# Layer 0's attention scores: float32r halves stacked over 128 rows, or float32 products on 32-row quarters

## The chip, the cores and the metric

The kernel runs on one core of one Trainium2 chip. The metric is the device time of one execution in microseconds. The kernel before was run three times: median 3027.15 us, 3026.36 to 3032.22. The profile is of one more execution, of 3024.22 us.

## What is computed

The input is x of 2 images, 256 channels, 64 x 64 points (4096 positions). Two layers follow one another, each with a group normalisation ahead of it and its result added to its input. The change touches layer 0 alone: an attention of 8 heads with 32 channels each over all 4096 positions.

```
qkv = einsum('bchw,oc->bohw', x, qkv_w) + qkv_b      # x: normalised
q, k, v = qkv.reshape(b, 3, 8, 32, 4096) ...
attn_logits  = einsum('bhci,bhcj->bhij', q, k) / sqrt(32)
attn_weights = softmax(attn_logits, axis=-1)
out = einsum('bhij,bhcj->bhci', attn_weights, v)
```

Layer 1 (windowed attentions, a 3 x 3 convolution) is the same in both kernels.

## The kernel before

**Stages.** For each image b: `project0` (L424) makes queries, keys and values on TensorE and puts them into DRAM; `attention0` (L494) is layer 0's attention; then layer 1. TensorE's, ScalarE's and VectorE's (DVE's) order inside `attention0` is the order in which the program writes the instructions (`manual_schedule`).

**Groups, blocks, units.** The attention of one image has 16 groups g: head h = g // 2, and half p = g % 2 of the 4096 queries. A group goes over 32 blocks j of 128 keys. For one block there are four units u of 512 queries each. A unit is one tile of scores, 128 keys by 512 queries, and there are 2048 units per image.

**Scores.** `heads4` (L426) writes each query and key twice to DRAM: rounded to float32r (ScalarE), and what the rounding left over (DVE, L439). `fetch_head` (L401) lays both parts of the keys over four row quarters of 32 partitions, `fetch_queries` (L411) both parts of the queries, so that one float32r product with 128 rows of contraction sums all four part-products. `scores` (L558) does nine units at a time in groups of 1, 1, 3, 2 and 2 (`PHASE`), each unit into one bank of a ring of seven PSUM banks; ScalarE takes the exponential of each group in one instruction (L573) into a ring of 28 places in SBUF. `touch` (L528) tells the scheduler which banks do not overlap.

**Weighted sums.** `quarters` (L578, matmul at L582) multiplies one block's exponentials with its values: four products of 32 output columns, one for each unit, onto four column quarters of the array, into the 32-partition quarters of one bank `av`. All blocks but the first and the last are done in two steps of 256 columns. These are plain float32.

**Row sums of the exponentials.** DVE adds each block's exponentials to two running tiles (`add_rows`, L597, addition at L619). For seven blocks of a group (`SUMMED`, L480) the addition is made by DMAs that accumulate in memory instead (`add_in_memory`, L621, issued by GpSimd at L627 and L629), and DVE adds their result at the start of the next group (L832). At a group's end `sum_rows` (L643) sums over the partitions by a product with ones into a spare bank of the ring; for the last group of an image the last four blocks are also summed so.

**Finish.** `finish` (L654) copies the row sums out (ScalarE, L660), takes their reciprocal through DRAM, and multiplies the copied weighted sums (ScalarE copy, L846). It is taken up at later blocks of the next group (`steps`, L810).

**Order.** The loop at the end of `attention0` puts out nine scores, then as many half-block steps of weighted sums as keep the ring in balance, then nine scores again.

Of the kernel before, what the change touches and what calls it, by code (L numbers as in the profile page):

```python
# [18 lines left out]
P = 128  # L19
# [22 lines left out]
def direct_layers(ctx: ExitStack, tc: tile.TileContext, a: dict, out: bass.AP, bad: bass.AP):  # L42
# [338 lines left out]
    def normalise(dst, src, k, mean, rstd):  # L381
# [9 lines left out]
    halves = {  # L391
        nm: [dram.tile([2, C, N], F32, name=f"{nm}_halves_{b}") for b in range(B)] for nm in ("wq0", "wk0")
    }
# [7 lines left out]
    def fetch_head(b, h, held):  # L401
        r = slice(HD0 * h, HD0 * h + HD0)
        kt = kpool.tile([P, N], F32R, tag="kv", name=f"k_{b}_{h}")
        for g in range(4):
            nc.sync.dma_start(
                out=kt[HD0 * g : HD0 * g + HD0, :].bitcast(F32), in_=halves["wk0"][b][g // 2, r, :]
            )
        held["k", h] = kt
        nc.sync.dma_start(out=held["v"][:, h % 2, :, :], in_=vals[b][:, :, r])

    def fetch_queries(b, g, held):  # L411
        h, p = divmod(g, 2)
        r = slice(HD0 * h, HD0 * h + HD0)
        for w in range(2):
            qt = w4([P, 2, T], f"q_{b}_{g}_{w}", F32R)
            n0 = (4 * p + 2 * w) * T
            for q in range(4):
                nc.sync.dma_start(
                    out=qt[HD0 * q : HD0 * q + HD0].rearrange("p s n -> p (s n)").bitcast(F32),
                    in_=halves["wq0"][b][q % 2, r, n0 : n0 + 2 * T],  # L420
                )
            held["q", g, w] = qt

    def project0(b, xn, w0):  # L424

        def heads4(nm, g):  # L426
            for t in range(NT):
                nt = f"{nm}_{b}_{g}_{t}"
                n = slice(t * T, (t + 1) * T)
                final = b > 0 and (nm, g, t) == ("wq0", KC - 1, NT - 1)  # L430
                pq = bank([P, T], f"p_{nt}", at=7 if final else None)
                for k in range(KC):
                    nc.tensor.matmul(  # L433
                        pq, w0[nm][:, k, g * P : (g + 1) * P], xn[:, k, n], start=k == 0, stop=k == KC - 1
                    )
                pair = w4([P, 2, T], f"hl_{nt}", F32R)
                bias = b0[nm][:, g : g + 1]
                nc.scalar.activation(pair[:, 0, :], pq, AF.Identity, bias=bias)
                nc.vector.scalar_tensor_tensor(  # L439
                    pair[:, 1, :], pq, bias, pair[:, 0, :].bitcast(F32), ALU.add, ALU.subtract  # L440
                )
                nc.sync.dma_start(
                    out=halves[nm][b][:, g * P : (g + 1) * P, n].rearrange("s p n -> p s n"),
                    in_=pair.bitcast(F32),
                )
# [3 lines left out]
        for i in range(N // P // 4):  # L449
# [19 lines left out]
            "acc": place[:, n_v + n_es : n_v + n_es + T].unsqueeze(1),  # L469
        }  # L470
        fetch_head(b, 0, held)
        fetch_queries(b, 0, held)
# [5 lines left out]
    RING, RING_A = 28, 17  # L478

    SUMMED = (3, 7, 11, 15, 18, 22, 26)  # L480

    def summed(g):

        return SUMMED if g else SUMMED[1:]


# [5 lines left out]
    RING_SHIFT = 3  # L492

    def attention0(b, xts, held):  # L494
# [5 lines left out]
        es = apool.tile([P, RING_A + 1, T], F32, tag="A", name=f"es_{b}")  # L500
        pair = cpool.tile([P, 2, T], F32, tag="col", name=f"acc_{b}")

        acc = [es[:, RING_A, :], held["acc"][:, 0, :], pair[:, 0, :], pair[:, 1, :]]
        vals2 = held["v"]
        n_units = NH0 * 2 * NJ * 4
        sums, added, copied = {}, {}, {}
        waiting = []
        last = NH0 * 2 - 1

        places = []  # L510
        n_places = 0

        def at_places(first, n):

            while n > 0:
                at = (first + RING_SHIFT) % RING
                m = min(n, (RING_A if at < RING_A else RING) - at)
                yield m, es[:, at : at + m, :] if at < RING_A else held["es"][:, at - RING_A : at - RING_A + m, :]
                first, n = first + m, n - m

        BANKS = 7

        PHASE = (1, 1, 3, 2, 2)
        recent, spare = [], [0]
        rows_made = ([], [])
        ring = psum["sc"].tile([P, BANKS, T], F32, tag="ring", name=f"ring_{b}")

        def touch(made, banks):  # L528

            for engine, past, other in recent:
                if engine != made.ins.engine and not banks & other:
                    tc.declare_no_dep(made.ins, past.ins, reason="another bank of the ring")
            recent.append((made.ins.engine, made, banks))
            del recent[:-60]
            return made

        def touch_spare(made):
            return touch(made, {spare[0]})  # L540

        def spare_bank():

            nonlocal n_places
            n_places += 1
            spare[0] = (n_places - 1) % BANKS
            return ring[:, spare[0], :]

        def runs_of(n):

            at = n_places
            while n > 0:
                e = (at + RING_SHIFT) % RING
                m = min(n, BANKS - at % BANKS, (RING_A if e < RING_A else RING) - e)
                yield at, m
                at, n = at + m, n - m

        def scores():  # L558

            nonlocal n_places  # L560
            for size in PHASE:
                for at, m in list(runs_of(min(size, n_units - len(places)))):
                    sc = ring[:, at % BANKS : at % BANKS + m, :]
                    for i in range(m):
                        unit = len(places) + i
                        g, (j, u) = unit // (4 * NJ), divmod(unit % (4 * NJ), 4)
                        touch(nc.tensor.matmul(  # L567
                            sc[:, i, :], held["k", g // 2][:, j * P : (j + 1) * P], held["q", g, u // 2][:, u % 2, :],
                            start=True, stop=True,
                        ), {at % BANKS + i})  # L570
                    ((_, dst),) = at_places(at, m)
                    touch(
                        nc.scalar.activation(dst, sc, AF.Exp, scale=SC0), set(range(at % BANKS, at % BANKS + m))  # L573
                    )
                    places.extend(range(at, at + m))
                    n_places = at + m

        def quarters(dst, lhs, rhs, start, stop, part=None, note=lambda made: made):  # L578

            n = slice(0, T) if part is None else slice(part * T // 2, (part + 1) * T // 2)  # L580
            for u in range(4):
                note(nc.tensor.matmul(dst[HD0 * u : HD0 * u + HD0, n], lhs, rhs(u)[:, n], start=start, stop=stop))  # L582

        def unit(g, j, u):
            ((_, e),) = at_places(places[(g * NJ + j) * 4 + u], 1)
            return e[:, 0, :]

        def two_units(g, j, w):

            one, two = (places[(g * NJ + j) * 4 + 2 * w + s] for s in range(2))  # L590
            if two == one + 1:
                runs = list(at_places(one, 2))
                if len(runs) == 1:
                    return [(slice(0, 2), runs[0][1])]
            return [(slice(s, s + 1), unit(g, j, 2 * w + s).unsqueeze(1)) for s in range(2)]

        def add_rows(g, j):  # L597
            if j == 0:
                sums[g] = psum["av"].tile([P, T], F32, tag="av", name=f"av_{b}_{g}")
                added[g] = [w4([P, 2, T], f"e_{b}_{g}_{w}") for w in range(2)]  # L600
                return
            for w in range(2):
                dst = added[g][w]
                if j in summed(g):
                    if w == 0:
                        add_in_memory(g, j)
                    continue
                if j == 1:
                    first = two_units(g, 0, w), two_units(g, 1, w)
                    if len(first[0]) == len(first[1]) == 1:  # L610
                        nc.vector.tensor_add(dst, first[0][0][1], first[1][0][1])
                    else:
                        for s in range(2):
                            nc.vector.tensor_add(dst[:, s, :], unit(g, 0, 2 * w + s), unit(g, 1, 2 * w + s))
                    continue
                for s, src in two_units(g, j, w):
                    if g == last and j in SUMMED_LAST:
                        continue
                    nc.vector.tensor_add(dst[:, s, :], dst[:, s, :], src)  # L619

        def add_in_memory(g, j):  # L621
            assert not waiting or j != summed(g)[0]
            runs = [(acc[u].unsqueeze(1), unit(g, j, u).unsqueeze(1)) for u in (0, 1)]
            runs += [(pair[:, s, :], src) for s, src in two_units(g, j, 1)]
            for dst, src in runs:
                if j == summed(g)[0]:
                    nc.gpsimd.dma_start(out=dst, in_=src)  # L627
# [1497 lines left out]
```

## Time and profile before

| what | value |
|---|---|
| median of 3 runs | 3027.15 us |
| profiled execution | 3024.22 us |
| its span on the core | 3022.4 us |
| attention of image 0, first score to last weighted sum | 111.46 to 1132.29 us |
| attention of image 1 | 1607.40 to 2633.80 us |
| TensorE clock granted | 0.998 of full speed |

The page of a profile gives first each engine's busy time, then the chain of work that ended last (shares of the span), then the costliest groups of instructions: line, engine, operation, output and inputs, shape (of a matmul first rows times columns of the array that it uses), count, busy time and mean ns of one, then idle time before them. PE is TensorE, PEld its weight loads, ACT is ScalarE, POOL is GpSimd. TensorE's ends are modelled, so the starts tell more than the busy time. A float32 product has two records there, a float32r product one.

### The profile page before, as it was taken

Reading aid. Unit: us, or ns where it says so; the run is one execution under the profiler, and the core shown is the slowest. Engines: PE = TensorE matmul, PEld = TensorE weight load, DVE = VectorE, ACT = ScalarE, POOL = GpSimd, SP = SyncE. Lnnn points to the kernel's source line nnn. Section 1 sums busy time; section 2 is a strip of 40 time slices with the busy share of each in tenths; the row PEclk is TensorE's granted clock in tenths of the full one; section 3 lists DMA queues with packets and bytes.
Section 4 is the critical chain, followed back from the end, with each engine's and each line's share of the span. In section 5 each row is a group of like instructions: output and inputs, shape, how many; then the busy total and the mean of one; then the engine's idle time right before and its main releaser. Section 6 shows DMA issues by size and latency. Waiting matters only on the chain.

```text
span 3022.4 us, 64069 instructions
## 1 busy us (share of the span) xinstructions
PE 2963.0 (98%) x25161; PEld 1850.1 (61%) x25161; DVE 2443.4 (81%) x3111; ACT 2341.5 (77%) x3288; POOL 843.3 (28%) x930
## 2 busy tenths in 40 slices
PE   7999999999999999999999999999999999999998
PEld 4565556665565656577765555666555565576765
DVE  4698998999899999856647989989988899935543
ACT  2699999999999994622237999999999999844333
POOL 1022222322223230065401223222222222306440
PEclk9999999999999999999999999999999999999999
DMA  7979779897897761230169688797888976700000
GB/s 263 278 138 183 148 158 173 158 185 155 169 179 156 157 137 36 76 141 31 49 222 265 131 172 166 158 178 148 172 169 161 185 159 128 175 13 4 22 15 23
DMA packets 246662, 425.55 MB, mean 141 GB/s; under 512 B 99096, under 2 KB 110156, under 8 KB 244172
## 3 DMA queue, kind: packets, MB, share of 16 engines
q0 software_dynamic: 96960, 237.57, 40.8%
q1 hardware_dynamic: 149244, 183.51, 22.0%
q8 instruction: 199, 3.26, 0.5%
q14 instruction: 115, 0.94, 0.1%
q10 hardware_dynamic: 144, 0.26, 0.0%
HBM read 120.08 MB, written 68.39 MB: 62 GB/s over the span
## 4 chain that ended last, share of the span: by engine, by line
PE 87%; DVE 5%; DMA 3%; ACT 2%; issue 1%; SPq 0%; ACTq 0%; DVEq 0%; POOLq 0%
PE ring L567 32%; PE av L582 29%; PE mm L1036 7%; PE p_wk L433 2%; PE pv L456 2%; PE p_wq L433 2%; DVE prep L957 2%; PE prq_sr L1417 2%; PE prk_sr L1417 2%; PE pvs_sr L1106 2%; PE phk_sr L1406 1%; PE phq_sr L1406 1%; PE ring L582 1%; PE pvs_lr L1106 1%; PE py L1243 1%
## 5 line engine op out<-in xcount | busy, mean ns | idle before, releaser
L573 ACT ACTIVATE es<-ring 128x512 f32<-128x512 f32 (+2 forms) x1574 | 1202.3, 909 | 35.4 <-PE ring L567 23.3
L567 PE MATMUL ring<-q,k 128*128 128x512 f32 x4096 | 1083.9, 407 | 7.3 <-ACT es L573 5.4
L619 DVE TENSOR_TENSOR e<-e,es 128x1024 f32<-128x1024 f32 (+1 forms) x942 | 1028.8, 1153 | 28.4 <-ACT es L573 27.4
L567 PEld LDWEIGHTS ring<-q,k 128*128 128x128 f32 x4096 | 731.2, 188 | 382.7 <-ACT es L573 116.4
L573 ACT ACTIVATE v<-ring 128x512 f32<-128x512 f32 (+2 forms) x1036 | 785.6, 896 | 15.6 <-PE ring L567 7.5
L582 PE MATMUL av<-es,v 128*32 128x256 f32 (+1 forms) x9648 | 722.1, 389 | 0.0
L619 DVE TENSOR_TENSOR e<-e,v 128x1024 f32<-128x1024 f32 (+1 forms) x624 | 669.1, 1128 | 18.3 <-ACT v L573 17.6
L582 PE MATMUL av<-v 128*32 128x256 f32 x6224 | 506.0, 389 | 0.0
L582 PEld LDWEIGHTS av<-es,v 128*32 128x32 f32 x9648 | 325.2, 109 | 263.8 <-issue 105.1
L582 PEld LDWEIGHTS av<-v 128*32 128x32 f32 x6224 | 222.2, 109 | 169.8 <-issue 70.3
L1036 PE MATMUL mm<-v,wf 128*128 128x256 f32 x1024 | 227.6, 380 | 2.0 <-DVE z L1047 2.0
L629 POOL DMA_DIRECT2D es<-es x116 | 99.0, 853 | 438.5 <-ACT es L573 412.7
L1036 PEld LDWEIGHTS mm<-v,wf 128*128 128x128 f32 x1024 | 192.9, 190 | 33.7 <-issue 6.9
L1026 POOL TENSOR_TENSOR v<-col 128x512 f32<-128x512 f32 x128 | 165.3, 1317 | 172.8 <-ACT rk_sr L1195 40.3
L629 POOL DMA_DIRECT2D acc<-es x126 | 129.5, 1033 | 116.4 <-ACT es L573 32.1
L1043 ACT COPY z<-mm 128x512 f32<-128x512 f32 x32 | 18.7, 585 | 179.1 <-PE mm L1036 179.1
L627 POOL DMA_DIRECT2D es<-es x20 | 11.4, 568 | 508.6 <-ACT es L573 241.1
L629 POOL DMA_DIRECT2D es<-v x74 | 63.1, 853 | 291.1 <-ACT v L573 265.6
L1044 DVE TENSOR_TENSOR z<-z,mm 128x512 f32<-128x512 f32 x32 | 21.9, 686 | 125.3 <-ACT z L1043 124.9
L629 POOL DMA_DIRECT2D v<-es x114 | 115.3, 1011 | 24.7 <-ACT es L573 8.9
L629 POOL DMA_DIRECT2D acc<-v x86 | 87.5, 1017 | 81.9 <-DMA acc<-es 35.5
L1022 POOL TENSOR_TENSOR col<-xp 128x1152 f32<-128x1152 f32 x32 | 69.3, 2165 | 66.6 <-DVE xp L1487 55.4
(252 smaller groups left out, 2639.2 us busy)
## 6 DMA issues: line engine op xcount, KB each, us to landing
acc<-es POOLq DMA_DIRECT2D x122, 512.0 KB, 6.3
acc<-v POOLq DMA_DIRECT2D x78, 512.0 KB, 6.2
es<-es POOLq DMA_DIRECT2D x136, 256.0 KB, 4.2
v<-es POOLq DMA_DIRECT2D x134, 256.0 KB, 5.3
k<-wk_halves SPq DMA_DIRECT2D x64, 512.0 KB
q<-wq_halves SPq DMA_DIRECT2D x256, 128.0 KB
v<-v POOLq DMA_DIRECT2D x88, 256.0 KB, 4.8
es<-v POOLq DMA_DIRECT2D x86, 256.0 KB, 3.9
```

Source lines behind the costliest of these rows:

```text
L433: nc.tensor.matmul(pq, w0[nm][:, k, g * P : (g + 1) * P], xn[:, k, n], start=k == 0, stop=k == KC - 1)
L456: nc.tensor.matmul(pv[:, j, :], xn[:, k, n0 : n0 + P], w0["wv0"][:, k, :], start=k == 0, stop=k == KC - 1)
L567: touch(nc.tensor.matmul(sc[:, i, :], held["k", g // 2][:, j * P : (j + 1) * P], held["q", g, u // 2][:, u % 2, :], start=True, stop=True, ...
L573: nc.scalar.activation(dst, sc, AF.Exp, scale=SC0), set(range(at % BANKS, at % BANKS + m))
L582: note(nc.tensor.matmul(dst[HD0 * u : HD0 * u + HD0, n], lhs, rhs(u)[:, n], start=start, stop=stop))
L619: nc.vector.tensor_add(dst[:, s, :], dst[:, s, :], src)
L629: nc.gpsimd.dma_start(out=dst, in_=src, accum_op=ALU.add)
L1022: (nc.gpsimd.tensor_add if plus else nc.gpsimd.tensor_sub)(col, cols(one), cols(two))
L1026: (nc.gpsimd.tensor_add if plus else nc.gpsimd.tensor_sub)(dst, rows(one), rows(two))
L1036: nc.tensor.matmul(mm[:, m, r, :], wf[:, k, 4 * r + q, m * P : (m + 1) * P], v[r // 2][:, r % 2, k, :], start=k == 0, stop=k == KC - 1,)
L1106: nc.tensor.matmul(pv[:, i, :], tokens(c, 2 * half + i), wv[:, c, :], start=c == 0, stop=c == KC - 1)
L1417: nc.tensor.matmul(pr[m], wts[two][:, k, m * P : (m + 1) * P], hid[:, k, :], start=k == 0, stop=k == KC - 1)
```

## The change

The scores become plain float32 products with 32 rows of contraction. `heads4` writes queries and keys once, ScalarE and DVE in turn, in pairs of 512 columns. `fetch_head` lays the same 32 key rows on all four row quarters, and on quarter u the queries of unit u, for both halves of the queries at once; `fetch_queries` is gone. `scores` does runs of three units, each unit on its row quarter and into its own bank, alternately into two PSUM tiles of three banks, with one exponential per run. The ring in SBUF has 30 places in fixed order.

The accumulating DMAs are gone. For 11 of 32 blocks (7 in an image's last group) TensorE adds the row sums, by products with ones like the weighted sums, into a bank of their own, `rows`; DVE adds the other blocks as before. The copies out of the weighted and the row sums move from ScalarE to DVE. The loop puts out one run of three, then up to 2.2 steps on average, while there are steps to take.

```diff
     def fetch_head(b, h, held):
...
-        kt = kpool.tile([P, N], F32R, tag="kv", name=f"k_{b}_{h}")
-        for g in range(4):
+        kt = kpool.tile([P, N], F32, tag="kv", name=f"k_{b}_{h}")
+        qt = w4([P, 2, T], f"q_{b}_{h}")
+        for u in range(4):
+            rows = slice(HD0 * u, HD0 * u + HD0)
+            nc.sync.dma_start(out=kt[rows, :], in_=heads["wk0"][b][r, :])
             nc.sync.dma_start(
-                out=kt[HD0 * g : HD0 * g + HD0, :].bitcast(F32), in_=halves["wk0"][b][g // 2, r, :]
+                out=qt[rows], in_=heads["wq0"][b][r, :].rearrange("c (p u n) -> c p u n", p=2, u=4)[:, :, u, :]
             )
...
-                pair = w4([P, 2, T], f"hl_{nt}", F32R)
+                if t % 2 == 0:
+                    pair = w4([P, 2, T], f"pair_{nt}")
                 bias = b0[nm][:, g : g + 1]
-                nc.scalar.activation(pair[:, 0, :], pq, AF.Identity, bias=bias)
-                nc.vector.scalar_tensor_tensor(
-                    pair[:, 1, :], pq, bias, pair[:, 0, :].bitcast(F32), ALU.add, ALU.subtract
-                )
...
+                if t % 2 == 0:
+                    nc.scalar.activation(pair[:, 0, :], pq, AF.Identity, bias=bias)
+                else:
+                    nc.vector.tensor_scalar(pair[:, 1, :], pq, bias, None, ALU.add)
...
-    RING, RING_A = 28, 17
-    SUMMED = (3, 7, 11, 15, 18, 22, 26)
+    RING, RING_A = 30, 18
+    RING_SHIFT = 18
+    RUN = 3
...
+    def by_ones(g):
+        return (14, 16, 18, 20, 22, 24, 26) if g == NH0 * 2 - 1 else (6, 9, 11, 14, 16, 19, 21, 24, 26, 30, 31)
...
+        runs = [psum["sc"].tile([P, RUN, T], F32, tag=f"run{i}", name=f"run{i}_{b}") for i in range(2)]
...
+        def scores(i):
+            sc, first = runs[i % 2], RUN * i
+            n = min(RUN, n_units - first)
+            for s in range(n):
+                g, (j, u) = (first + s) // (4 * NJ), divmod((first + s) % (4 * NJ), 4)
+                rows = slice(HD0 * u, HD0 * u + HD0)
+                nc.tensor.matmul(
+                    sc[:, s, :], held["k", g // 2][rows, j * P : (j + 1) * P], held["q", g // 2][rows, g % 2, :],
+                    start=True, stop=True,
+                )
+            nc.scalar.activation(places(first, n), sc[:, 0:n, :], AF.Exp, scale=SC0)
...
+            if j in by_ones(g) or (g == last and j in SUMMED_LAST):
+                return
             for w in range(2):
...
+                nc.vector.tensor_add(
+                    added[g][w], two_units(g, 0, w) if j == 1 else added[g][w], two_units(g, j, w)
+                )
...
+            if j == NJ - 1 and g < last:
+                avs = copied[g] = w4([P, 2, T], f"avs_{b}_{g}")
+                nc.vector.tensor_copy(avs[:, 0, :], sums[g])
+            if j in by_ones(g):
+                begins = j == by_ones(g)[0]
+                if begins:
+                    rows_of[g] = psum["rows"].tile([P, T], F32, tag="rows", name=f"rows_{b}_{g}")
+                for part in (None,) if begins else range(2):
+                    yield
+                    quarters(rows_of[g], ones, lambda u: unit(g, j, u), begins, False, part)
...
-            touch_spare(nc.scalar.copy(avs[:, 1, :], rows))
+            nc.vector.tensor_copy(avs[:, 1, :], rows_of[g])
...
-            per_group = 2 * NJ - 2
-            behind, reach = 7, sum(PHASE) + 1
-            work, begun, taken = steps(), 0, 0
+            work, begun, made, owed = steps(), 0, 0, 0.0
+            per_run = 2.2
             while begun < NH0 * 2 * NJ:
-                scores()
+                scores(made)
+                made += 1
+                final = RUN * made >= n_units
+                ready = NH0 * 2 * NJ if final else RUN * (made - 2) // 4
...
+                owed = min(owed + per_run, 4.0) if begun < ready else 0.0
```

In the changed kernel the score matmul stands at L501 and the matmul of `quarters` at L511.

## The prediction

> **What bounds the kernel now.** I read the page's busy shares first, then its chain, then the busy times of the two stretches that the change touches, and last the records of TensorE inside them. On the page:
>
> ```profile
> PE 2963.0 (98%) x25161; PEld 1850.1 (61%) x25161; DVE 2443.4 (81%) x3111; ACT 2341.5 (77%) x3288; POOL 843.3 (28%) x930
> ...
> PE ring L567 32%; PE av L582 29%; PE mm L1036 7%; PE p_wk L433 2%; PE pv L456 2%; PE p_wq L433 2%; DVE prep L957 2%; PE prq_sr L1417 2%; PE prk_sr L1417 2%; PE pvs_sr L1106 2%; PE phk_sr L1406 1%; PE phq_sr L1406 1%; PE ring L582 1%; PE pvs_lr L1106 1%; PE py L1243 1%
> ...
> L573 ACT ACTIVATE es<-ring 128x512 f32<-128x512 f32 (+2 forms) x1574 | 1202.3, 909 | 35.4 <-PE ring L567 23.3
> L567 PE MATMUL ring<-q,k 128*128 128x512 f32 x4096 | 1083.9, 407 | 7.3 <-ACT es L573 5.4
> L619 DVE TENSOR_TENSOR e<-e,es 128x1024 f32<-128x1024 f32 (+1 forms) x942 | 1028.8, 1153 | 28.4 <-ACT es L573 27.4
> ...
> L582 PE MATMUL av<-es,v 128*32 128x256 f32 (+1 forms) x9648 | 722.1, 389 | 0.0
> ```
>
> 61% of the span's chain is the score products (L567) and the weighted sums (L582): layer 0's attention, on TensorE. Busy time alone proves little there (ends are modelled), and ScalarE is nearly full as well in these stretches (the busy times of the two attentions, first score to last weighted sum):
>
> ```profile
> core 0: us, PE busy (x) PEld busy (x) DVE busy (x) ACT busy (x) POOL busy (x), PEclk, DMA share, GB/s
> 111.46:1132.29 1020.83, 1017.72 (x10207) 607.45 (x10207) 947.78 (x966) 991.18 (x1349) 289.47 (x347) 1.00 0.81 165
> 1607.40:2633.80 1026.40, 1020.09 (x10205) 607.20 (x10204) 949.11 (x968) 990.48 (x1347) 285.96 (x347) 1.00 0.81 164
> ```
>
> Together 2047.2 us; ACT 97%, DVE 93%. So what TensorE really needs must come from its starts. Three timelines of TensorE give the prices (columns: start us, length us):
>
> ```profile
> 596.86 0.41 PE L582 MATMUL av<-v 128*32 128x256 f32 x2
> 596.87 0.41 PE L582 MATMUL av<-es,v 128*32 128x256 f32 x2
> 597.10 0.39 PE L582 MATMUL av<-v 128*32 128x256 f32 x2
> 597.11 0.39 PE L582 MATMUL av<-es,v 128*32 128x256 f32 x2
> 597.31 0.39 PE L582 MATMUL av<-v 128*32 128x256 f32 x2
> ...
> 599.15 2.33 PE L567 MATMUL ring<-q,k 128*128 128x512 f32 x9
> 601.41 1.71 PE L582 MATMUL av<-es,v 128*32 128x256 f32 x27
> ```
> ```profile
> 1146.98 1.45 PE L1243 MATMUL py<-es,wt_g 128*128 128x512 f32 x3
> 1148.36 1.92 PE L1257 MATMUL pa<-es,w_at 128*32 128x512 f32 x16
> 1150.21 0.70 PE L1106 MATMUL pvs_lr<-wt_w,es 128*128 128x256 f32 x2
> ```
>
> - A float32 product shows as two records, each half of it: L433 has 128 records for 64 products, one every 429 ns, so 858 ns for 512 columns. A float32r product of 512 columns is one record; inside a burst they start 226 to 236 ns apart, 227 where nothing waits.
> - The four quarters of a weighted sum start together, within 0.02 us, and the next four 0.216 us later (256 columns; 0.429 for 512). Four column quarters really run at once.
> - Changing the shape costs. Third py (1146.98 + 2 x 0.429 = 1147.84) to first pa is 0.52, 0.09 more than 0.429, and the next group comes 0.024 late (a 32-column weight load). Back, the last group (1149.67) to 1150.21 is 0.54, 0.11 more, and the second 128-column product 0.104 late. A round trip costs about 0.34 us, for the float32r bursts too.
>
> Check: 599.15 to 603.28, the next burst, holds 9 scores, 8 groups and one round trip: 9 x 0.227 + 8 x 0.216 + 0.34 = 4.11 us; the trace has 4.13. TensorE is the bound, ScalarE just behind.
>
> **What the Trainium skill says.** "TensorEngine Tiling (Array Packing)", Key Properties: changing the tiling mode drains TensorE; the 0.34 us agrees. "FP8 and Floating Point Precision", TensorE Precision Notes: true float32 takes four passes; the trace's 858 against 227 ns agrees. "TensorE: Matmul & The Clock Gate", LDWEIGHTS: a load is timed by columns, not rows; the trace has about 109 ns for 32 columns, 188 for 128, both of 128 rows. Same page, Part 3: matmuls on different row quarters run together, four at 3.07 times the rate of one, three column quarters at 2.38 times. For columns the trace does better (four for the price of one); for 32-row quarters of 128 columns the trace has nothing.
>
> **The change, part by part.** Counts are of the two batches, in the order of the built programs.
>
> 1. *Scores.* Removed: 4096 float32r products x 0.227 = 929.8 us. Added: 4096 float32 products in 1366 runs of three (one of each batch shorter). If the quarters run together a run costs one product, 0.858: 1172.0 us. Bounds: below, one half-record instead of two (0.43), which L1138 speaks against: five rows of contraction, and still some 52 ns per 64 columns and half-record, the same rate as 429 for 512. Above, three in series, 2.574.
> 2. *Row sums by TensorE.* Weighted sums are unchanged at 7680 quarter products of 256 columns and 256 of 512. Row sums go from 96 and 120 to 2496 and 288 (11 of 32 key blocks per group, 7 in the last). Each group of four is two half-records: before, 7776/4 x 2 x 0.2157 = 838.6 and 376/4 x 2 x 0.4292 = 80.7; after, 10176/4 x 2 x 0.2157 = 1097.5 and 544/4 x 2 x 0.4292 = 116.7. Plus 294.9 us.
> 3. *Mode changes.* Bursts of nine (454 round trips) become runs of three (1260; 100 stretches hold more than one run). Before 454 x 0.34 = 154.4; after 1260 x 0.35 (0.01 more, as three starts lie 7 ns apart) = 441.0. The row quarters' loads have no row: free when covered, as by columns, or two more 128-column loads exposed per trip, 2 x 0.104. I take covered.
> 4. *What is lifted off the others.* The accumulating DMAs, and their issues on GpSimd, go (575 us of its busy time). DVE's additions fall to 20 blocks x 2 x 1.215 us per group: 32 x 48.6 = 1555 us, with some 40 us of copies taken from ScalarE. ScalarE: 1366 exponentials of 1536 at 1.51 us at most, 2063 us. All lie under TensorE's new sum, so they bring nothing. Added waits: the copy out of the weighted sums' only bank (0.62 us on ScalarE, L846) moves behind DVE's additions, and the next group's first weighted sum waits for it. DVE has half its time free and block 31 has no additions; TensorE meanwhile has that block's row sums and the next run (2 us). The row-sum bank's copy has from block 2 to block 6 of the next group. SP loses the query fetches per group (eight of 128 KB) and writes half as much; heads are still fetched a head ahead, under 2 x 80 us of work. I cost these at zero; were the fetches late, about 10 us a head would show.
> 5. *Projection.* Half the bias writes on ScalarE and DVE go, but TensorE runs there at 13.73 us per 16 products, exactly 0.858 each: no gain.
>
> Sum for the attentions: before 929.8 + 838.6 + 80.7 + 154.4 = 2003.5, against 2047.2 measured, so 44 us are waits (start-up, ScalarE's fullness, the tail). After 1172.0 + 1097.5 + 116.7 + 441.0 = 2827.2, and with ScalarE slack I leave 20 of the 44: 2847. Difference +800 us, all on the path. The profiled execution took 3024.2 (span 3022.4), so 3824; the median lies 3 above it: 3827, rounded to **3825 us**.
>
> **Rivals.**
> - *Loads of the row quarters serialise, or the packing is poorer than by columns.* Plus 1260 x 0.21 = 265: 4090; by the page's 2.38 for three tiles (an estimate: 3/2.38 = 1.26), 0.26 x 1172 = 305: 4130.
> - *Mode changes between row and column quarters are cheaper.* At zero: 3825 - 441 = 3384; half price 3605. Against it: the drain shows at every change of shape in the trace.
> - *The quarters do not overlap: the change doesn't do what it says.* In series 1366 x 1.716 more: 6170; overlapping only second with first halves (four half-records instead of two), 1366 x 0.858 more: 5000. Against it: the columns do overlap. For it: no row-quarter row exists, and the second half of one product stands ahead of the next in program order.
> - *Faster: the small products are cheap, and ScalarE was the bound.* Break-even is a run with its share of a round trip at (2047 - 20 - 1214)/1366 = 0.595 us; I count 1.18. Only one half-record per product (0.43) and nearly free mode changes get below. Then ScalarE's 1366 exponentials (1.33 apart in a 1536 burst) bind at about 1820: 2820. For it: ACT at 97%. Against it: L1138.
>
> **How the numbers follow.** Likeliest case 0.60 (own range 3760 to 3890), loads or packing 0.16, cheap mode changes 0.12, no overlap 0.09, faster 0.03. Half the cheap-mode case lies above 3600; the packing case reaches 4130. So 3600 to 4130 leaves out some 0.18. About 0.2% is what a measurement of this kernel can tell from no change. Faster 0.03, same 0.01, slower 0.96.
>
> **What would show it.** Right: three L501 score records within 0.02 us, three more 0.43 us later, then a 0.5 us step into L511; ACT near 70%, POOL near idle in the attention; each attention near 1424 us. Step 1 is wrong if second and third scores start 0.43 us or more after the first; step 3 if the steps differ from 0.52 and 0.54; step 2 if row-sum groups are not 0.216 apart. A TensorE idle for exponentials, keys or copies would break step 4.

## The result and the profile after

| what | before | after |
|---|---|---|
| median | 3027.15 us (3 runs, 3026.36 to 3032.22) | 3812.06 us (4 runs, 3807.93 to 3813.14) |
| profiled execution, its span | 3024.22, 3022.4 | 3807.93, 3806.1 |
| the two attentions | 2047.2 us | 2828.3 us |
| the rest of the span | 975.2 us | 977.8 us |

The ratio is 1.2584, 95% interval 1.256 to 1.2609: the changed kernel is a quarter slower. Predicted were 3825 us, range 3600 to 4130. A fourth execution of the kernel before took 15540 us, why is not known; it is left out of the median and of the ratio. Nearly all of the loss lies in the two attentions (2828.3 - 2047.2 = 781 of 784 us).

The page of the changed kernel, for the lines shown of before (L501 is the score product, L505 its exponential, L511 the quarter products, L527 VectorE's addition):

```profile
PE 3749.1 (99%) x34393; PEld 1638.5 (43%) x34393; DVE 2155.2 (57%) x2691; ACT 2323.9 (61%) x1948; POOL 282.1 (7%) x242
...
PE run L501 38%; PE av L511 27%; PE rows L511 10%; PE mm L914 6%; PE p_wk L421 1%; PE pv L445 1%; PE p_wq L421 1%; DVE prep L835 1%; PE prk_sr L1295 1%; PE prq_sr L1295 1%; PE pvs_sr L984 1%; PE phk_sr L1284 1%; PE phq_sr L1284 1%; PE pvs_lr L984 1%; PE py L1121 1%; PE pc_sr L1060 1%
...
L501 PE MATMUL run<-q,k 32*128 32x512 f32 x8192 | 1522.0, 638 | 4.5 <-ACT v L505 4.5
L505 ACT ACTIVATE es<-run 128x1536 f32<-128x1536 f32 x816 | 1177.6, 1451 | 507.6 <-PE run L501 497.4
L527 DVE TENSOR_TENSOR e<-e,es 128x1024 f32<-128x1024 f32 x730 | 868.1, 1221 | 509.9 <-ACT es L505 507.8
...
L511 PE MATMUL av<-es,v 128*32 128x256 f32 (+1 forms) x9504 | 735.3, 391 | 0.0
```

There are twice as many score records (8192 for 4096), 10% of the chain is in the new row sums, and ScalarE and VectorE now sit idle for 0.5 ms each before the lines shown (ScalarE until TensorE's scores come, VectorE until ScalarE's exponentials). The busy times of the two attentions say the same (columns as in the prediction):

```profile
111.21:1526.61 1415.40, 1412.60 (x14822) 501.87 (x14822) 812.89 (x770) 992.31 (x692) 4.75 (x2) 1.00 0.12 27
2003.85:3416.77 1412.92, 1411.19 (x14821) 501.29 (x14820) 813.56 (x771) 990.33 (x689) 4.76 (x2) 1.00 0.12 26
```

ScalarE's 992 us are those of before (991), in a window of 1415 instead of 1021: 70%. VectorE is at 57%, GpSimd idle, and DMA engines are 12% busy instead of 81%. None of it shortened the attentions.

TensorE's timeline in the steady part (start us, length us; x3 is three records together, two answers put into one fence):

```profile
601.55 0.40 PE L511 MATMUL av<-es,v 128*32 128x256 f32 x4
601.88 0.70 PE L501 MATMUL run<-q,k 32*128 32x512 f32 x3
...
602.42 0.60 PE L501 MATMUL run<-q,k 32*128 32x512 f32 x3
602.95 0.42 PE L511 MATMUL rows<-es,ones 128*32 128x256 f32 x4
```

The first halves of a run's three products start together at 601.88, the second halves together 0.53 us later (0.429, and 0.104 that I read as the exposed weight load), the first quarter group another 0.53 later (0.429 and the drain, the wait at the change of shape). Three row quarters run at once, and their loads as well: the three start within 0.014 us and take 0.181 us each. Over all records, a run of three takes 1.064 us from its first score to the next quarter product (median of 1160), two runs back to back 1.916 (of 96), four groups of quarter products 1.001 until the next score. So a round trip (a run and the return to scores, beyond the products themselves) costs (1.064 - 0.858) + (1.001 - 4 x 0.2157) = 0.206 + 0.138 = 0.344 us. I had 0.35.

### The profile page after: what moved, and what is told of

Same layout as the page of the kernel before. It is cut to its first block, busy times and chain, and to the rows that moved or that the text cites. A ratio compares the mean times of both kernels' runs of the same rounds, so it can differ in the third digit from the quotient of the medians.

```text
span 3806.1 us, 77613 instructions
## 1 busy us (share of the span) xinstructions
PE 3749.1 (99%) x34393; PEld 1638.5 (43%) x34393; DVE 2155.2 (57%) x2691; ACT 2323.9 (61%) x1948; POOL 282.1 (7%) x242
## 4 chain that ended last, share of the span: by engine, by line
PE 94%; DVE 3%; ACT 1%; DMA 1%; issue 0%; SPq 0%; POOL 0%; ACTq 0%
PE run L501 38%; PE av L511 27%; PE rows L511 10%; PE mm L914 6%; PE p_wk L421 1%; PE pv L445 1%; PE p_wq L421 1%; DVE prep L835 1%; PE prk_sr L1295 1%; PE prq_sr L1295 1%; PE pvs_sr L984 1%; PE phk_sr L1284 1%; PE phq_sr L1284 1%; PE pvs_lr L984 1%; PE py L1121 1%; PE pc_sr L1060 1%
## 5 line engine op out<-in xcount | busy, mean ns | idle before, releaser
L501 PE MATMUL run<-q,k 32*128 32x512 f32 x8192 | 1522.0, 638 | 4.5 <-ACT v L505 4.5
L505 ACT ACTIVATE es<-run 128x1536 f32<-128x1536 f32 x816 | 1177.6, 1451 | 507.6 <-PE run L501 497.4
L527 DVE TENSOR_TENSOR e<-e,es 128x1024 f32<-128x1024 f32 x730 | 868.1, 1221 | 509.9 <-ACT es L505 507.8
L505 ACT ACTIVATE v<-run 128x1536 f32<-128x1536 f32 (+1 forms) x550 | 792.2, 1449 | 335.8 <-PE run L501 328.7
L527 DVE TENSOR_TENSOR e<-e,v 128x1024 f32<-128x1024 f32 x486 | 579.1, 1221 | 344.6 <-ACT v L505 343.4
L511 PE MATMUL av<-es,v 128*32 128x256 f32 (+1 forms) x9504 | 735.3, 391 | 0.0
L501 PEld LDWEIGHTS run<-q,k 32*128 32x128 f32 x8192 | 434.5, 183 | 596.5 <-issue 487.7
L511 PE MATMUL av<-v 128*32 128x256 f32 (+1 forms) x6368 | 519.3, 392 | 0.0
L511 PEld LDWEIGHTS av<-es,v 128*32 128x32 f32 x9504 | 272.5, 109 | 549.4 <-issue 442.8
L511 PEld LDWEIGHTS av<-v 128*32 128x32 f32 x6368 | 189.9, 109 | 367.9 <-issue 296.2
L511 PE MATMUL rows<-es,ones 128*32 128x256 f32 (+1 forms) x3184 | 265.8, 397 | 0.0
L511 PE MATMUL rows<-v,ones 128*32 128x256 f32 (+1 forms) x2128 | 186.4, 397 | 0.0
L511 PEld LDWEIGHTS rows<-es,ones 128*32 128x32 f32 x3184 | 93.2, 109 | 177.9 <-issue 138.1
L511 PEld LDWEIGHTS rows<-v,ones 128*32 128x32 f32 x2128 | 64.8, 109 | 118.5 <-issue 92.1
```

What stands on the lines that cost most here:

```text
L501: nc.tensor.matmul(sc[:, s, :], held["k", g // 2][rows, j * P : (j + 1) * P], held["q", g // 2][rows, g % 2, :], start=True, stop=True,)
L505: nc.scalar.activation(places(first, n), sc[:, 0:n, :], AF.Exp, scale=SC0)
L527: nc.vector.tensor_add(added[g][w], two_units(g, 0, w) if j == 1 else added[g][w], two_units(g, j, w))
```

## The experiments

The theory is the prediction's sum: TensorE's starts add up, scores, quarter products and mode changes. The rivals are named in each expectation.

**One record a score.** The changed kernel, the score product alone exchanged. Of the edit two lines are shown; the rest are the casts that go with it and the scale of the exponential.

```diff
-        kt = kpool.tile([P, N], F32, tag="kv", name=f"k_{b}_{h}")
+        kt = kpool.tile([P, N], F32R, tag="kv", name=f"k_{b}_{h}")
...
-                    sc[:, s, :], held["k", g // 2][rows, j * P : (j + 1) * P], held["q", g // 2][rows, g % 2, :],
+                    sc[:, s, :], held["k", g // 2][:, j * P : (j + 1) * P], held["q", g // 2][:, g % 2, :],
```

> The changed kernel with the score product alone exchanged: one float32r product over all 128 rows for each unit, in the same runs of three and the same order. It sums the four row quarters of keys and queries, so the scores are not the reference's (a quarter of the sum is taken), and nothing is rounded in two parts. Theory (TensorE's starts add up: scores + quarter products + mode changes): scores 4096 x 0.227 = 930 instead of 1172 us, round trips 1260 x 0.34 instead of 0.35, so 255 us less than 3812: 3557. Rival (most of the loss lies in the order of runs and row sums, and float32 row quarters are as cheap as float32r): within 30 of 3812. Rival (row quarters cost more than one product at a time): under 3480.

Measured: 3579.63 us, ratio to before 1.1828 (1.1808 to 1.1848). That is 232 less than the changed kernel. The rival of cheap row quarters falls, and so does that of dear ones. The 23 us short of the theory are in the price of the float32r product and in the trip: a run of three takes 0.892 us in this trace (median of 1160), against 3 x 0.227 + 0.206 = 0.887 in my sum; and with products 0.23 us apart, as inside longer bursts, the round trip is about 0.34 for both kinds, where I gave row quarters 0.01 more. 1160 x (1.064 - 0.892) + 96 x (1.916 - 1.589) = 231 us is the whole difference.

**Few row sums on TensorE.**

```diff
-        return (14, 16, 18, 20, 22, 24, 26) if g == NH0 * 2 - 1 else (6, 9, 11, 14, 16, 19, 21, 24, 26, 30, 31)
+        return (14,) if g == NH0 * 2 - 1 else (6, 31)
```

> The changed kernel with row sums by TensorE for 2 of 32 blocks of a group instead of 11 (1 instead of 7 in the last), the rest added by VectorE. Theory: quarter products 971 instead of 1214 us, round trips 1082 instead of 1260 (62 us), together 305 less: 3507; VectorE's additions rise to 32 x 30 x 2 x 1.22 = 2343 us plus about 100 of other work, under the attentions' 2523, so it is nearly full and 0 to 60 us may come back. Rival (VectorE becomes the bound, its additions wait for exponentials and the ring): 3600 or more. Rival (row sums lie under other work): 3812.

Measured: 3511.05 us, ratio 1.1599 (1.1579 to 1.1618): 301 less than the changed kernel. VectorE takes the additions over, without holding anyone up. Its busy time in the attentions (third pair) rises from 813 to 1117 of some 1265 us:

```profile
112.69:1380.27 1267.58, 1264.85 (x12566) 452.82 (x12566) 1117.44 (x1052) 982.83 (x692) 4.32 (x2) 0.99 0.13 29
1859.60:3119.64 1260.04, 1258.58 (x12565) 451.44 (x12564) 1117.93 (x1053) 980.99 (x689) 4.32 (x2) 1.00 0.13 29
```

So with scores this slow, most row sums on TensorE were not needed: VectorE had the time.

**Two runs a burst.**

```diff
-                scores(made)
-                made += 1
+                for _ in range(2):
+                    if RUN * made < n_units:
+                        scores(made)
+                        made += 1
...
-            per_run = 2.2
+            per_run = 4.4
...
-                owed = min(owed + per_run, 4.0) if begun < ready else 0.0
+                owed = min(owed + per_run, 8.0) if begun < ready else 0.0
```

> The changed kernel with two runs of three scores put out together and twice as many steps after them: the same work in 680 instead of 1260 round trips between row quarters and column quarters. Theory (a round trip costs 0.35 us): 580 x 0.35 = 203 less: 3609. Rival (the second run waits for its bank, since the exponential of the run two before has not ended): at most half of that gain, above 3700. Rival (mode changes are not what costs): 3812.

Measured: 3669.19 us, ratio 1.2125 (1.2105 to 1.2146): 143 less, between the theory and its rival. Of 676 bursts of two runs 484 take 1.916 us, but 192 take 2.18 or more; the mean is 2.002, and 676 x (2.002 - 1.916) = 58 us, nearly the 60 that are missing. In all 192 the second run starts 0.052 to 0.053 us after an exponential has ended. TensorE's list of waits names the exponentials too (PEld is the weight load; us in total, times, longest; 300 to 1000 us of each span): first the changed kernel, then this one.

```profile
PEld run L501 <- ACT es L505: 17.3, 41, 0.8
PEld run L501 <- ACT v L505: 6.5, 15, 0.8
```
```profile
PEld run L501 <- ACT es L505: 43.0, 68, 0.9
PEld run L501 <- ACT v L505: 26.1, 41, 0.9
```

The wait for exponentials triples. A score product shares only its PSUM bank with them, so it is the bank that is waited for. Loads overlap running products, so the size of the loss is read from the lengths of the bursts. Mode changes cost what I said, and what is saved on them is partly paid back with two PSUM tiles.

These bursts show one thing more. In 236 of them the first product of the second run, on the row quarter that the first run leaves free, starts 0.26 us after the first one, while three others are running, and their second halves come no later for it (0.533 us). One such burst, up to 0.06 and up to 0.36 us from its start:

```profile
1945.44 0.70 PE L501 MATMUL run<-q,k 32*128 32x512 f32 x3
1945.44 0.95 PE L501 MATMUL run<-q,k 32*128 32x512 f32 x4
```

So four row quarters run at once as well. The changed kernel's runs of three leave one of them empty: a score costs 0.858/3 = 0.286 us, with four it would be an estimated 0.858/4 = 0.2145, less than the 0.23 of float32r. Two tiles of four banks would need eight, as many as the kernel uses in all (six, `av` and `rows`). This was not tried.

**All scores on one row quarter.**

```diff
-                rows = slice(HD0 * u, HD0 * u + HD0)
+                rows = slice(0, HD0)
```

> The changed kernel with all scores on the first row quarter, so that the three products of a run cannot run together (they then use the queries of unit 0 for all units, so the scores are not the reference's). Theory (the three row quarters really ran at once, a run costs one product of 0.858): 1366 x 1.716 = 2344 more: 6156. Rival (they ran in part one after another): less than that, by what they already lost[...].

Measured: 10187.55 us, ratio 3.3686 (3.3572 to 3.3799), far over both. Two things are in it. At full clock a run is what the theory says: after the first, the first scores of the span start 0.429 us apart (113.830, 114.259, 114.688, 115.117), one half-product after the other, and the shortest twentieth of the runs take 2.767 us, 6 x 0.429 and the drain. But about 2 us in, the clock falls: from 115.547 on the starts are 0.853 apart, twice as far. The busy times show the clock granted in the attentions (third number from the end), and the timeline a run of 5.4 us instead of 2.77:

```profile
113.30:4688.95 4575.65, 4575.65 (x14822) 1548.14 (x14822) 823.53 (x770) 997.98 (x692) 6.26 (x3) 0.55 0.04 8
5164.82:9785.24 4620.42, 4620.42 (x14821) 1562.37 (x14820) 824.27 (x771) 996.25 (x689) 6.06 (x3) 0.54 0.04 8
```
```profile
601.11 1.94 PE L511 MATMUL av<-es,v 128*32 128x256 f32 x16
602.97 5.49 PE L501 MATMUL run<-q,k 32*128 32x512 f32 x6
608.39 1.94 PE L511 MATMUL rows<-es,ones 128*32 128x256 f32 x16
```

(2828 + 2344)/0.55 = 9404 us; the attentions took 9196. So the packing is priced here by those few runs at full clock, not by the total.

**Scores on two row quarters.**

```diff
-                rows = slice(HD0 * u, HD0 * u + HD0)
+                rows = slice(HD0 * (u % 2), HD0 * (u % 2) + HD0)
```

> The changed kernel with the scores on two row quarters in turn (units 0 and 2 on the first, 1 and 3 on the second, with the queries of units 0 and 1, so the scores are not the reference's). Each run of three then has two products on one quarter. Theory (a run costs as many products as its busiest quarter has): 1366 x 0.858 = 1172 more than 3812: 4984, at full clock. Rival (the clock granted falls when few rows of the array are in use, as it did to about 0.55 with one quarter): 6000 to 9000. Rival (products on different quarters share something and are not worth a full product each): between 4984 and 6156 at full clock.

Measured: 4962.51 us, ratio 1.6381 (1.6299 to 1.6463). A run takes 1.909 us (median of 1160), two products in turn, 0.845 more than with three quarters. Two runs back to back (96 of them) take 2.774, three products. So a stretch of scores costs as many products as its busiest quarter holds: the packing is worth its full price.

That the total comes so near the theory's 4984 is luck. Runs back to back share products, which the theory forgot: 1160 x 0.845 + 96 x 0.858 = 1063 us more, not 1172. And the clock does fall, for a while at the start of each attention (third number from the end), 229 us at half clock in all, an estimated 114 us lost:

```profile
115.80:167.00 51.20, 50.41 (x186) 16.06 (x186) 16.79 (x14) 18.04 (x13) 0.00 (x0) 0.50 0.25 48
167.00:2085.05 1918.05, 1917.38 (x14627) 720.18 (x14624) 804.05 (x756) 972.29 (x676) 6.05 (x3) 1.00 0.08 18
2566.60:2744.10 177.50, 177.50 (x708) 56.67 (x706) 40.71 (x34) 49.33 (x34) 0.00 (x0) 0.50 0.07 13
```

3808 + 1063 + 114 = 4985; the profiled execution took 4986.

The Trainium skill's page "TensorE: Matmul & The Clock Gate", Part 3, measured 3.07 times the rate of one for four row quarters. Here three alone give (2.767 - 0.206)/0.858 = 2.98 times, with the 2.767 us of the experiment before; the measurement decides.

**The kernel before in bursts of three.** The mode changes tested in the other kernel.

```diff
-        PHASE = (1, 1, 3, 2, 2)
+        PHASE = (1, 2)
```

> The kernel before with bursts of three scores (exponentials of one and two) instead of nine: 1318 instead of 454 round trips, all else the same. Theory (0.34 us each, on TensorE's path): 864 x 0.34 = 294 more, of which ScalarE's waits give back up to 40: 3285 to 3325. Rival (round trips hide behind ScalarE, which is 97% busy): 3030 to 3080, from the smaller exponentials alone (0.460 instead of 0.455 us a unit).

Measured: 3299.93 us, ratio 1.091 (1.0893 to 1.0926): 274 more. Round trips do not hide behind ScalarE, though it is 97% busy in the kernel before. In this trace a burst of three takes 0.893 us, as in the first experiment.

**The kernel before without most accumulating DMAs.** Only the first of seven blocks goes to memory; the rest is left out of the row sums.

```diff
                 if j == summed(g)[0]:
                     nc.gpsimd.dma_start(out=dst, in_=src)
-                else:
-                    nc.gpsimd.dma_start(out=dst, in_=src, accum_op=ALU.add)
```

> The kernel before without the accumulating DMAs: of the seven blocks of a group that are summed in memory only the first is fetched, the other six are left out of the row sums (the output is not the reference's). Theory (these DMAs and their issues on GpSimd lie off the path, so their removal is worth nothing): 3020 to 3035. Rival (they slow the engines' access or hold places of the ring): 2990 or less, and the change gave that much back.

Measured: 3016.44 us, ratio 0.9968 (0.9958 to 0.9979): 10 us less, just outside the theory's range (3020 to 3035) and far from the rival's. GpSimd's busy time in the attentions falls from 575 to 65 us and the DMA share from 0.81 to 0.26, and TensorE hardly notices. The sums in memory were nearly free. The changed kernel pays some 300 us of TensorE's time for such sums, 11 blocks of a group instead of seven.

**Longer bursts for the kernel before.** If round trips cost 0.34 us, bursts of more than nine should beat both kernels. Four kernels, each with one of these added lines:

```diff
-        PHASE = (1, 1, 3, 2, 2)
+        PHASE = (1, 1, 3, 2, 3)          # ten
+        PHASE = (2, 2, 3, 2, 2)          # eleven
+        PHASE = (2, 3, 2, 3, 2)          # twelve
+        PHASE = (2, 2, 3, 2)             # nine, wider exponentials
```

> The kernel before with bursts of eleven scores, exponentials of 2, 2, 3, 2 and 2 units: 372 instead of 454 round trips, and 0.450 instead of 0.455 us of ScalarE a unit. Theory: 82 x 0.34 = 28 less: 3000. Rival (seven banks are too few for eleven scores, TensorE waits for exponentials inside the burst): 3030 or more.

> The kernel before with bursts of twelve scores, exponentials of 2, 3, 2, 3 and 2 units: 340 instead of 454 round trips. Theory: 114 x 0.34 = 39 less: 2990. Rival (the banks are too few, TensorE waits inside the burst): 3030 or more.

> The kernel before with bursts of ten scores in exponentials of 1, 1, 3, 2 and 3 units: 408 instead of 454 round trips. Theory (0.34 us each): 16 less, 3010. Rival (seven banks are too few beyond nine, TensorE waits inside the burst): 3060 or more.

> The kernel before with its nine scores in exponentials of 2, 2, 3 and 2 units instead of 1, 1, 3, 2 and 2: one instruction less in nine units for ScalarE (0.449 instead of 0.455 us a unit), TensorE's work unchanged. Theory (TensorE's starts are the bound): 3026, within 10. Rival (ScalarE's time is the bound): 2000 x 0.006 x 2 = 20 less, 3005. Rival (wider groups hold their banks longer, so that TensorE waits inside the burst, as with eleven and twelve): 3060 or more.

Measured: eleven 3218.81 (ratio 1.0642, 1.0628 to 1.0657), twelve 3311.2 (1.0946, 1.0931 to 1.0961), ten 3293.89 (1.0886, 1.0871 to 1.0901), nine with wider exponentials 3109.7 (1.0273, 1.0259 to 1.0287). All four of my theories fell, and the rival with the banks holds. The waits of TensorE on exponentials (300 to 1000 us, as above), before and with ten:

```profile
PEld ring L567 <- ACT es L573: 37.8, 95, 0.8
PEld ring L567 <- ACT v L573: 22.7, 56, 0.8
...
PE ring L567 <- ACT v L573: 0.2, 1, 0.2
```
```profile
PEld ring L567 <- ACT es L573: 72.7, 85, 1.2
...
PEld ring L567 <- ACT v L573: 42.8, 49, 1.2
...
PE ring L567 <- ACT es L573: 40.0, 65, 0.8
PE ring L567 <- ACT v L573: 24.2, 39, 0.8
```

A burst of nine takes 2.276 us before (median), 2.516 with wider exponentials; ten take 3.45, eleven 3.42. The loss is inside the bursts: those of ten are 3.256 long on average, and 404 x (3.256 - 2.276 - 0.23) = 303 us, less 17 that the kernel before loses in the same way and 16 for 46 trips saved, is 270; measured are 267. The sum of starts is a floor, not a forecast: it holds only as long as a bank is free for each start. Why ten is worse than eleven (the order of exponentials differs too) was not tried. No version here that makes all the sums beats the kernel before.

## Why the prediction was right

- *The bound.* TensorE's starts, as said. Sum for the attentions after: 2827.2 predicted, 2828.3 measured. That it fits to 1 us is luck: with the measured 0.344 a trip the sum is 2819.6, which leaves 9 us of waits, where I had added 20. Of the 44 us that I took for waits before, some 12 are the price of the float32r product (next point). Most of the 13 us by which 3825 is high is in the 20.
- *Step 1, scores.* 242 us predicted, and 13 of the mode changes' rise for the row quarters' trips. Undone alone: 232. Two terms were mis-sized: float32r products are 0.23 us apart in the burst of nine ((2.276 - 0.206)/9), not 0.227, and the row quarters' trip (0.344) costs hardly more than the other (about 0.34). The two half-records and the overlap of three quarters hold; that the second halves come 0.53 us after the first, where I named 0.43 as the sign, is the 0.104 of the trip.
- *Step 2, row sums.* 295 us predicted; undoing most of them with their round trips gives 301, where 305 were expected.
- *Step 3, mode changes.* 0.35 us a trip predicted, 0.344 measured, and +274 us when the kernel before is given 864 more. The loads of three row quarters are covered, as I chose.
- *Step 4, what is lifted off the others.* Nearly nothing, as said: 10 us for the DMAs, where I had zero. TensorE's waits on VectorE come to 7 us in image 0's attention, so the copies that moved to VectorE's queue are no new bound.
- *Step 5, projection.* The time outside the attentions changed by 2.6 us.
- *Rivals.* Serial loads, poorer packing and no overlap: excluded by the starts, and by a run on two quarters taking 0.845 us more. Cheap mode changes: excluded by bursts of three. The faster case needed 0.595 us for a run with its trip; it is 1.18.

## What to carry to other kernels

Price a change to a full TensorE by its starts: records per product, how many quarters really run together, and every change of shape, of which small runs have many. Relief on other engines is worth little while TensorE ends last: here 10 us for nearly all the accumulating DMAs. Splitting a contraction into row quarters only restores what the smaller contraction leaves unused, and it depends on filling them: a float32 product of two records with three of four quarters filled (0.286 us a score) loses to one float32r record over all rows (0.23); with four filled it need not. A saving on round trips needs free banks first.

## What the runs showed of the hardware that I had not expected

With all matmuls of the scores on one row quarter the clock granted to TensorE fell to half about 2 us after the first score, and was 0.55 of full speed on average through 4.6 ms, although TensorE's records leave no gap there: starts of 0.853 instead of 0.429 us. The quarter products in between filled all rows, and did not bring it back for long.

The fall itself is not particular to one quarter. The changed kernel, with three, has it some 4 us after its first score as well, but there it lasts 3.4 us:

```profile
115.40:118.80 3.40, 3.40 (x12) 1.05 (x12) 1.23 (x2) 2.62 (x2) 0.00 (x0) 0.51 1.04 222
```

With two quarters it lasted 51 and 177 us. With one the clock was at half for 91% of the first attention, at full speed for only 3 to 27 us at a time. So in these three profiles the clock stayed down longer, the fewer quarters the scores filled; by what rule it is granted, they do not show.
